# A four-layer graph network: layer 1 and the input norm moved forward, low lanes weighed on ScalarE, searches further ahead

## The chip, the core and the metric

The kernel runs on one core of a Trainium2 chip. It is launched once and computes all 16 graphs. The metric is the device time of that launch in microseconds (us). Engines carry the names of the profile: PE is TensorE (matmuls; PEld are its weight loads), DVE is VectorE, ACT is ScalarE, POOL is GpSimd and SP is SyncE. In this kernel POOL issues only indirect DMAs (a gather or scatter of 128 rows by a column of indices) and SP issues all other DMAs.

## The reference

Sixteen graphs of 1024 nodes and 64 features, each with a weighted adjacency matrix, go through four layers. Every layer adds its output to its input, and begins with `h = max(layernorm(x), 0)`.

```python
# layer 0
out = einsum('bij,bjo->bio', adj, h @ weight) + bias
# layer 1
e = f_src[:, :, None] + f_dst[:, None, :]      # from leaky_relu(h @ W) @ a
dj = 0.8 * adj + 0.2 * e
attention = softmax(where(dj > 0, dj, -1e12), axis=1)
out = relu(einsum('bij,bjo->bio', attention, h @ W))
# layer 2 (hyperbolic attention)
x_local = logmap(x_i, x_j, c)
att = sigmoid(einsum(..., att_W) + att_b) * adj
out = proj(expmap(einsum('bij,bijd->bid', att, x_local), x, c), c)
# layer 3: quantiles over the neighbours that are left after thinning
s = sort(where(nd[..., None], h[:, None, :, :], inf), axis=2)
agg = 0.25 * q(0.25) + 0.5 * q(0.5) + 0.25 * q(0.75)   # between two sorted lanes each
out = (relu((h + agg) @ W1 + b1) @ W2 + b2) * mask
```

Layer 3 is the unusual one. Each node has a list of neighbours whose features are sorted, one feature apart from the other, and three quantiles are read from the sorted list.

## The kernel before, in words

**Streams and a planner.** The kernel is written as generators ("streams") that issue instructions. A planner runs while the program is built. It books each instruction on a model of the engines (`Plan`), and at each point it steps the stream that is ready and least far in its share of VectorE work. `yield [tile]` means "go on when the plan has this tile finished", `yield (tile,)` the same and 12 us later (`LATE_US`), and `yield lambda: ...` waits for a state of another stream. These waits exist only while building; what the chip sees is a fixed order for each engine, recorded in `Queue.call` at L190, so that nearly every instruction of the profile has line L190 and is told by its tiles. On the chip, real semaphores hold each instruction until its tiles are there.

**heads** (`heads`, `fast0`, `fast1`, `fast2`) goes over the graphs. `fast0` is layer 0: norm, then for 8 column tiles of the adjacency matrix the matmuls `pa<-adj,h`, and the edge flags `ng<-adj` on VectorE. `fast1` is layer 1: its norm, transposes and small matmuls (the preamble), and then the attention over 8 tiles (`d<-adj,fsr,fd`, `ex`). `fast2` is layer 2: 16 half-row units of pairs (`pd`, `pl` on PE, `u_g` and `u_z` on ScalarE and VectorE, transposes `pw`, `w<-pw,adj`, and `pm`). **moves** then makes the step of layer 2 (`move_steps`, some 40 tiny VectorE instructions that begin with `dot_pr` and `c_hm`), stores x and the norm for layer 3 (`s_hd`) in DRAM, and raises `headed`. `heads` of the next graph does its layer 0 meanwhile, but waits for `headed` ahead of all of layer 1, as layer 1's tiles take the memory of the step's (`moving.close()`).

**places** thins the edges, ranks each row's neighbours (a prefix sum on PE) and sorts the nodes by their number of neighbours. It scatters the rank rows, so sorted, to DRAM (`s_vp`, 8 indirect DMAs a graph on POOL). **weigh** makes the weight of each sorted lane (`wlow`, `wd`).

**fetches** finds the neighbours. For 128 nodes it loads rank rows (`row`, three buffers, two loads ahead), searches them on VectorE (`max_index`, FIND_INDEX8 in the profile) for eight ranks at once, and queues one gather from `s_hd` for each lane: 116 for the rows with few neighbours (`la`) and 48 for the 80 "hub" nodes (`hg`) a graph. What it looks for, 32 ranks for low rows or 8 for hubs, is copied by ScalarE behind the row's 1024 entries, so that a rank which the row lacks is found in the pad (it then gathers a row of zeros). `Issue` puts the queued gathers in POOL's order, and the scatters between them. `AHEAD_US = 16.0` says how far ahead of POOL's planned work a search is made. The first searches of a graph wait for `headed`.

**hubs** and **lows** sort by max and min on VectorE (`ha`/`hb`, `la`/`lb`), with copies of idle lanes on ScalarE. For low rows there are seven groups (`LOW`) of 31 to 7 lanes; after the sort VectorE multiplies the lanes that a quantile can touch by `wlow` (one instruction a group) and sums them in halves into `aggl`:

```python
v = a[:pn, :, l0:l1, :]
nc.vector.tensor_tensor(v, v, wlow[...].to_broadcast([pn, nt, l1 - l0, C]), ALU.mult)
```

**finish** stores the sums, gathers them back in node order (`ga`, 8 indirect DMAs on POOL), runs layer 3's two matmuls (`hid`, `py`) and stores the result.

Three states `st[b % 3]` bound how many graphs are under way. Streams share VectorE by `HEADS_US, HUBS_US, LOWS_US = 127.0, 82.0, 93.0`.

Of the kernel before, what the change touches and what calls it, by code (L numbers as in the profile page):

```python
# [29 lines left out]
C = 64  # L30
# [40 lines left out]
AHEAD_US = 16.0  # L71
LA = (1, 3, 2)
LATE_US = 12.0
HEADS_US, HUBS_US, LOWS_US = 127.0, 82.0, 93.0
PAD = 32
# [268 lines left out]
def tile_gnn_stack(  # L344
# [76 lines left out]
    seek = scp.tile([P, PAD], F16, name="seek")  # L421
    nc.gpsimd.iota(seek, pattern=[[2, PAD]], base=1, channel_multiplier=0, allow_small_or_imprecise_dtypes=True)
    iolane = scp.tile([P, 288], F32, name="iolane")
    nc.gpsimd.iota(iolane, pattern=[[1, 288]], base=0, channel_multiplier=0, allow_small_or_imprecise_dtypes=True)
    nseek = scp.tile([P, PAD], F32, name="nseek")
    nc.gpsimd.iota(nseek, pattern=[[-2, PAD]], base=-1, channel_multiplier=0, allow_small_or_imprecise_dtypes=True)
# [941 lines left out]
    def fast0(feed, xt, xn, ng):  # L1368

        with tc.tile_pool(name="f0", bufs=1) as sp, tc.tile_pool(name="f0p", bufs=1, space=PSUM) as ps:  # L1370
            h = sp.tile([P, NT, C], F32, name="h")
            yield from norm_steps(h, xt, sp, "ln_xc")
            pa = ps.tile([P, HN], F32, name="pa")
            po = ps.tile([P, 2, NT, C], F32, name="po")
            for hf in range(2):
                nc.tensor.matmul(po[:, hf, 0:4, :], ones[0:1, :], b0r[0:1, None, :].to_broadcast([1, 4, C]), start=True, stop=False)

            def others(J):
                blk = ng[:, J, J * P:(J + 1) * P]
                nc.vector.tensor_tensor(blk, blk, noteye, ALU.mult)  # L1380

            yield [h]
            for J in range(NT):
                a = feed.next()
                yield [a, h]
                halves(pa, h[:, J, :], a, J)
                nc.vector.tensor_scalar(ng[:, J, :], a, 0.0, None, ALU.is_gt)
                if J:
                    others(J - 1)
            others(NT - 1)  # L1390
            yield [pa]
            ga = sp.tile([P, HN], F32, name="ga")
            nc.scalar.copy(ga, pa)
            yield [ga]

            for k in range(4):
                for hf in range(2):
                    rs = slice(64 * hf, 64 * hf + 64)
                    nc.tensor.matmul(po[:, hf, k, :], ga[rs, k * P:(k + 1) * P], w0d[rs], start=False, stop=(k == 3))
            yield  # L1400
            v = "p (h k) c -> p h k c"
            nc.vector.tensor_tensor(xn.rearrange(v, h=2), po[:, :, 0:4, :], xt.rearrange(v, h=2), ALU.add)

    def fast1(feed, xt, xn):
        with tc.tile_pool(name="f1", bufs=1) as sp, tc.tile_pool(name="f1w", bufs=2) as wp, \
                tc.tile_pool(name="f1p", bufs=2, space=PSUM) as ps:
            h = sp.tile([P, NT, C], F32, name="h")
            yield from norm_steps(h, xt, sp, "ln_xc")

            cat = sp.tile([P, N], F32, name="cat")  # L1410
# [29 lines left out]
            hp = sp.tile([P, NT, C], F32, name="hp")  # L1440
            nc.scalar.copy(hp, ph)
            yield [fsr, fd]
# [67 lines left out]
            r = sp.tile([P, HN], F32, name="r")  # L1510
# [306 lines left out]

    def heads(io, feed, T, st):

        xa = load_x(io, 0)  # L1820
        moving = None
        for b in range(B):
            s = st[b % 3]
            nes = ExitStack()
            ng = nes.enter_context(tc.tile_pool(name="n1", bufs=1, side="right")).tile([P, NT, N], F16, name="ng")
            yield [xa]
            yield from fast0(feed, xa, xa, ng)
            T.flagged[b] = ng, nes.enter_context(tc.tile_pool(name="np", bufs=2, space=PSUM, side="right"))
            yield lambda: T.headed >= b
            if moving:  # L1830
                moving.close()
            yield [xa]
            yield from fast1(feed, xa, xa)
            yield [xa]

            def ranked():
                yield lambda: T.ranked > b
                nes.close()

            moving = ExitStack()  # L1840
            tp = moving.enter_context(tc.tile_pool(name="mv", bufs=1))
            args = yield from fast2(feed, xa, s.bad, ranked, tp)
            T.moves[b] = xa, args, moving.enter_context(tc.tile_pool(name="mw", bufs=1))
            if b + 1 < B:
                xa = load_x(io, b + 1)
            yield []
        yield lambda: T.headed >= B
        moving.close()
# [47 lines left out]
    def places(b, s, sp, T):  # L1896
# [119 lines left out]
        nc.vector.tensor_scalar(s.place, rk, float(N - 1), 0.5, ALU.add, ALU.mult)  # L2016
        for I in range(NT):
            issue.rows.append(lambda I=I: nc.gpsimd.indirect_dma_start(
                out=s.vp, out_offset=bass.IndirectOffsetOnAxis(ap=s.place[:, I:I + 1], axis=0),
                in_=vr[:, I, :], in_offset=None))  # L2020
# [158 lines left out]
    class Tail:  # L2179

        def __init__(self, es):
# [3 lines left out]
            self.dp = es.enter_context(tc.tile_pool(name="yd", bufs=2, space=bass.MemoryType.DRAM))  # L2185
            self.placed = self.ranked = self.headed = self.turned = self.hubbed = self.lowed = self.finished = 0
            self.out = [0, 0, 0]
            self.flagged, self.got, self.weights, self.sums, self.moves = {}, {}, {}, {}, {}

# [58 lines left out]
        def fetches(self, b, s):  # L2248
# [31 lines left out]
            def load():  # L2280
# [3 lines left out]
                row = wp.tile([P, N + PAD], F16, tag="row", name="row", bufs=3)  # L2284
                if i < 6:
# [12 lines left out]
                    nc.scalar.copy(row[:pn, N:N + 8], hseek[:pn, t, :])  # L2298
                else:
# [3 lines left out]
                    nc.scalar.copy(row[:pn, N:], seek[:pn])  # L2303
                rows[i] = row

            load()
            load()
# [26 lines left out]
            def search(row, n, what, pn):  # L2334
                ix = wp.tile([P, 8], U32, tag="ix", name="ix", bufs=8)
                nc.vector.max_index(ix[:pn], what, row[:pn, 0:n])
                return ix
# [6 lines left out]
            def fetch_hub(k):  # L2344
# [3 lines left out]
                for h in range(2):  # L2348
# [3 lines left out]
                    ix = search(rows[2 * k + h], N + 8, hseek[:pn, k, :], pn)  # L2352
# [4 lines left out]
            def fetch_low(k):  # L2357
# [5 lines left out]
                for t in range(t0, t0 + nt):  # L2363
# [3 lines left out]
                    yield lambda: len(issue.queue) <= 24  # L2367
# [9 lines left out]
                    for l0 in range(0, d, 8):  # L2377
                        if d - l0 <= 3:
                            yield [sm]
                            ix = wp.tile([P, 8], I32, tag="ix", name="ix", bufs=8)  # L2380
# [52 lines left out]
        def lows(self, b):  # L2433
# [3 lines left out]
            wlow = self.weights[b][0]  # L2437
            aggl = self.sums[b, 1] = self.bp.tile([P, LOWT, C], F32, name="aggl", bufs=2)
            for k, (t0, nt, d, few) in enumerate(LOW):
# [7 lines left out]
                v = a[:pn, :, l0:l1, :]  # L2447
                nc.vector.tensor_tensor(v, v, wlow[:pn, t0:t0 + nt, l0:l1][:, :, :, None].to_broadcast([pn, nt, l1 - l0, C]), ALU.mult)
                yield
# [6 lines left out]
                self.out[(k > 0) + (k > 4)] -= 1  # L2456
# [3 lines left out]
        def finish(self, b, s):  # L2460
# [19 lines left out]
            yield [ad]  # L2480
# [10 lines left out]
            hid = bp.tile([H, N], F32, name="hid")  # L2491
# [9 lines left out]
            for t in range(NT):  # L2501
                nc.tensor.matmul(py[:, t, :], hid[:, t * P:(t + 1) * P], w2s, start=False, stop=(t == NT - 1))
            yield [py]
# [50 lines left out]
    with ExitStack() as es:  # L2554
# [5 lines left out]
        def each(f, *more):  # L2560
            for b in range(B):
# [6 lines left out]
                  Stream(plan, each(lambda b: moves(b, st[b % 3], T)), lag=-1.0),  # L2568
                  Stream(plan, heads(io, Feed(io), T, st), HEADS_US),
# [67 lines left out]
```

## Time and profile before

| | |
|---|---|
| median of 23 runs | 5237.44 us (5214.2 to 5259.39) |
| profiled execution, its own time | 5231.94 us |
| its span, first to last instruction | 5230.2 us |
| mean granted TensorE clock | 0.597 |
| first edge flags (`ng<-adj`) of graphs 0, 1, 2, 15 | 33, 274, 530, 4500 us |
| first step instruction (`c_hm`) of graph 15 | 4786 us |
| gathers `la` and `hg`: first, last | 295, 5188 us |
| gathers `la` of graph 9 and of graph 10 begin | 3025, 3325 us |

Busy times are unions of records. A group's mean is the length of one record, and records of neighbouring instructions on an engine overlap by a little, so the distance from start to start is the better price when instructions follow each other closely; the prediction says which it uses. The first 500 us fill the pipeline: layer 3 of the first graph can't begin before its layer 2 is done. From about 530 to 4786 us graphs follow each other every 306 us, with layer 0 to 2 of one graph beside layer 3 of the one or two before. The last 440 us hold what is left of layer 3. "issue" behind an indirect DMA is time in which POOL waits for nothing that the profile shows. `DVE ix` as the releaser of a gather is the search that found its indices.

### The profile page before, as it was taken

What the parts mean: (1) busy time and instruction counts of PE and PEld (TensorE: products, weight loads), DVE (VectorE), ACT (ScalarE), POOL (GpSimd) and SP (SyncE); (2) the same over time, 40 slices, a digit from 0 to 9 for tenths busy, and PEclk for the clock granted to TensorE, in tenths of its full rate; (3) what the DMA queues carried; (4) which work ended last, traced back from release to release, by engine and by line L of the source; (5) the groups of instructions that cost most, each with busy time, mean ns of one, the idle gap of its engine ahead of it and who ended that gap; (6) DMA issues with size and microseconds to landing.
All of it is one profiled execution on the core that took longest, in us unless ns stands there. A gap on an engine that the chain in (4) does not pass through costs nothing. (4 is left out here: it accounts for less than half of the span.)

```text
span 5230.2 us, 59422 instructions
## 1 busy us (share of the span) xinstructions
PE 3470.0 (66%) x13331; PEld 1893.2 (36%) x13332; DVE 4679.7 (89%) x12742; ACT 3152.9 (60%) x9317; POOL 3810.5 (73%) x2906
## 2 busy tenths in 40 slices
PE   6967686766867567686866768686767867674010
PEld 2525243333524334352433435243343524333000
DVE  3368999899999999999999999989999999999866
ACT  4566666657566665756667575666757566675222
POOL 0057778788777777777777777777777777678886
PEclk8566656556565655656556565755666565665555
DMA  2133333333333233333333333332333333232120
GB/s 86 55 92 83 95 82 86 84 93 77 84 96 81 76 98 89 76 85 96 77 79 100 89 76 85 97 77 77 93 96 79 81 98 77 77 102 42 38 43 14
DMA packets 458515, 419.30 MB, mean 80 GB/s; under 512 B 215811, under 2 KB 349411, under 8 KB 458148
## 3 DMA queue, kind: packets, MB, share of 16 engines
q1 hardware_dynamic: 351652, 295.93, 19.5%
q0 software_dynamic: 106496, 119.49, 12.0%
q8 instruction: 108, 1.77, 0.1%
q14 instruction: 259, 2.12, 0.1%
HBM read 363.98 MB, written 50.54 MB: 79 GB/s over the span
## 5 line engine op out<-in xcount | busy, mean ns | idle before, releaser
L190 POOL DMA_INDIRECT la<-s_hd,ix x1856 | 2517.2, 1356 | 837.0 <-issue 489.8
L190 POOL DMA_INDIRECT hg<-s_hd,ix x768 | 1005.1, 1309 | 235.0 <-issue 208.5
L190 DVE TENSOR_TENSOR lb<-la 128x128 f32<-128x128 f32 (+14 forms) x1760 | 674.5, 434 | 65.8 <-DMA la<-s_hd,ix 43.8
L190 DVE TENSOR_TENSOR la<-lb 128x256 f32<-128x256 f32 (+11 forms) x1856 | 694.0, 428 | 32.1 <-ACT lb L190 26.9
L190 DVE TENSOR_TENSOR hb<-ha 128x128 f32<-128x128 f32 (+36 forms) x1632 | 655.2, 442 | 34.6 <-ACT ha L190 33.6
L190 DVE TENSOR_TENSOR ha<-hb 128x64 f32<-128x64 f32 (+36 forms) x1568 | 620.2, 435 | 21.9 <-ACT hb L190 21.3
L190 PE MATMUL pd<-near,dist 66*128 66x512 f32 x512 | 468.7, 1016 | 10.9 <-DVE u_g L190 6.3
L190 PE MATMUL pv<-wtile,krow 8*128 8x512 f16 x512 | 295.5, 577 | 249.0 <-ACT d L190 152.8
L190 PE MATMUL pl<-near,lead 65*128 65x512 f32 x512 | 459.5, 998 | 0.0
L190 PEld LDWEIGHTS pm<-hn,w 128*128 128x128 f32 x2048 | 431.0, 317 | 71.2 <-issue 59.0
L190 PE MATMUL pm<-hn,w 128*128 128x65 f32 x2048 | 435.7, 399 | 5.6 <-DVE w L190 5.6
L190 ACT ACTIVATE u_g<-pd,gxc 128x512 f32<-128x512 f32 x256 | 175.4, 685 | 317.9 <-PE pd L190 317.6
L190 PE MATMUL pw<-ident,u_z 128*128 128x128 f32 x1024 | 261.8, 407 | 158.0 <-DVE u_z L190 157.9
L190 POOL DMA_INDIRECT s_vp<-vr,s_place x128 | 147.3, 1150 | 266.5 <-DVE s_place L190 170.1
L190 PE MATMUL pa<-adj,h 128*64 128x512 f32 x512 | 163.3, 764 | 266.8 <-ACT h L190 210.4
L190 PEld LDWEIGHTS <-ng 128*128 128x128 f16 x2048 | 170.3, 127 | 467.8 <-issue 467.8
L190 ACT COPY ha<-hb 128x4 f32<-128x4 f32 (+22 forms) x1264 | 253.1, 273 | 119.9 <-DVE hb L190 90.8
L190 ACT COPY hb<-ha 128x32 f32<-128x32 f32 (+24 forms) x1280 | 272.5, 287 | 79.4 <-DVE ha L190 76.1
L190 ACT COPY lb<-la 128x64 f32<-128x64 f32 (+6 forms) x784 | 196.0, 298 | 181.5 <-DVE la L190 113.3
L190 PE MATMUL pv<-wt,ng 128*128 128x128 f16 x2048 | 301.9, 300 | 0.0
L190 ACT ACTIVATE u_z<-u_z,c_gs 128x512 f32<-128x512 f32 x256 | 183.4, 717 | 191.4 <-DVE u_z L190 187.7
L190 PEld LDWEIGHTS pw<-ident,u_z 128*128 128x128 f32 x1024 | 199.4, 226 | 248.9 <-issue 237.4
(300 smaller groups left out, 7901.0 us busy)
## 6 DMA issues: line engine op xcount, KB each, us to landing
adj<-in_adjt SPq DMA_DIRECT2D x384, 512.0 KB
la<-s_hd,ix POOLq DMA_INDIRECT x1856
row<-s_vp SPq DMA_DIRECT2D x112, 256.0 KB
hg<-s_hd,ix POOLq DMA_INDIRECT x768
wb<-wd SPq DMA_DIRECT2D x32, 342.0 KB
row<-s_vp SPq DMA_DIRECT2D x192, 28.0 KB
row<-s_vp SPq DMA_DIRECT2D x192, 24.0 KB
x<-in_x SPq DMA_DIRECT2D x16, 256.0 KB
```

The source lines that it names most:

```text
L190: r = f(*a, **k)
```

## The change

1. **Low lanes.** A new stream `totals` takes over from `lows`. For each group ScalarE multiplies every lane of every tile by its weight (a Copy ACTIVATE of 128x64 with a pointer scale), 79 a graph in place of 7 VectorE instructions; VectorE still makes the sums. Groups 1 to 6 are written to a new tile `lw`, of which there is one; a lock (`taken`) keeps it for one group at a time, and layer 3's hidden tile `hid` shares it. `LOWS_US` is 78.
2. **Searches.** `AHEAD_US` is 40, the queue may hold 40 gathers for low rows too (24 before), and there are 16 index buffers (8 before). Rows lie in four fixed tiles, three loads ahead. What is looked for is written behind each of them once, at the start: the hubs' 24 ranks and then the low rows' 32, so `PAD` is 56, a hub search reads 1048 entries (1032 before) and a low one 1080 (1056).
3. **Layer 1.** `fast1` takes its tiles from the other end of memory and calls `cleared()`, which waits for `headed`, only after the preamble and ahead of the attention. `hp` shares the buffer of `h`, and `r` that of `cat`.
4. **Input norm.** A new stream `first_norms` loads x and makes layer 0's norm ahead of `heads`.
5. `heads` waits ahead of layer 2 until graph b - 3 is finished; the scatters and the gathers of `finish` are queued 12 us later than the plan has their tiles.

```diff
-AHEAD_US = 16.0
+AHEAD_US = 40.0
...
-HEADS_US, HUBS_US, LOWS_US = 127.0, 82.0, 93.0
-PAD = 32
+HEADS_US, HUBS_US, LOWS_US = 127.0, 82.0, 78.0
+PAD = 56
+ROWS = 4
...
-    def fast0(feed, xt, xn, ng):
+    def fast0(feed, xt, xn, ng, h):
...
-            h = sp.tile([P, NT, C], F32, name="h")
-            yield from norm_steps(h, xt, sp, "ln_xc")
...
-    def fast1(feed, xt, xn):
-        with tc.tile_pool(name="f1", bufs=1) as sp, tc.tile_pool(name="f1w", bufs=2) as wp, \
+    def fast1(feed, xt, xn, cleared):
+        with tc.tile_pool(name="f1", bufs=1, side="right") as sp, ExitStack() as es, \
...
+            yield from cleared()
+            wp = es.enter_context(tc.tile_pool(name="f1w", bufs=2))
...
+    def first_norms(b, io, T):
+
+        yield lambda: T.headed >= b - 1 and T.entered >= b
+        xa = load_x(io, b)
+        yield [xa]
+        h = io.tile([P, NT, C], F32, name="h0")
+        yield from norm_steps(h, xa, io, "ln_xc")
+        T.normed[b] = xa, h
+        yield []
...
+            def cleared():
+                yield lambda: T.headed >= b
+                if moving:
+                    moving.close()
+
             yield [xa]
-            yield from fast1(feed, xa, xa)
+            yield from fast1(feed, xa, xa, cleared)
...
+            yield lambda: T.finished >= b - 2
             moving = ExitStack()
...
+        yield (s.place,)
...
+            self.rows = [self.bp.tile([P, N + PAD], F16, name=f"row{k}") for k in range(ROWS)]
+            for row in self.rows:
+                nc.vector.tensor_copy(row[:, N:N + 24], hseek.rearrange("p t l -> p (t l)"))
+                nc.vector.tensor_copy(row[:, N + 24:], seek)
...
-                    nc.scalar.copy(row[:pn, N:N + 8], hseek[:pn, t, :])
...
-                    nc.scalar.copy(row[:pn, N:], seek[:pn])
...
-            load()
-            load()
+            for _ in range(ROWS - 1):
+                load()
...
-                    ix = search(rows[2 * k + h], N + 8, hseek[:pn, k, :], pn)
+                    ix = search(rows[2 * k + h], N + 24, hseek[:pn, k, :], pn)
...
-                    yield lambda: len(issue.queue) <= 24
+                    yield lambda: len(issue.queue) <= 40
...
-                v = a[:pn, :, l0:l1, :]
-                nc.vector.tensor_tensor(v, v, wlow[:pn, t0:t0 + nt, l0:l1][:, :, :, None].to_broadcast([pn, nt, l1 - l0, C]), ALU.mult)
...
+        def totals(self, b):
...
+                if k:
+                    yield lambda: not self.taken
+                    self.taken = True
+                    o, s0 = self.bp.tile([P, nt * (l1 - l0) * C], F32, tag="lw", name="lw"), l0
+                    o = o.rearrange("p (t l c) -> p t l c", t=nt, c=C)
+                yield [a]
+                for i in range(nt * (l1 - l0)):
+                    t, l = i // (l1 - l0), l0 + i % (l1 - l0)
+                    nc.scalar.activation(o[:pn, t, l - s0, :], a[:pn, t, l, :], AF.Copy, scale=wlow[:pn, t0 + t, l:l + 1])
+                    if i % 8 == 7:
+                        yield []
...
-            yield [ad]
+            yield (ad,)
...
-            hid = bp.tile([H, N], F32, name="hid")
+            yield lambda: not self.taken
+            self.taken = True
+            hid = bp.tile([P, N], F32, tag="lw", name="hid")[:H]
...
+                  Stream(plan, each(T.totals), lag=-1.0),
+                  Stream(plan, each(lambda b: first_norms(b, io, T)), lag=-1.0),
```

## The prediction

> **What bounds the kernel now.** I read the page's busy line and slices first, then the waits of GpSimd and VectorE in the steady part (830 to 4790 us), then the timeline where one graph's gathers end and the next begin, and the groups by form for prices.
>
> ```profile
> PE 3470.0 (66%) x13331; PEld 1893.2 (36%) x13332; DVE 4679.7 (89%) x12742; ACT 3152.9 (60%) x9317; POOL 3810.5 (73%) x2906
> ...
> DVE  3368999899999999999999999989999999999866
> ACT  4566666657566665756667575666757566675222
> POOL 0057778788777777777777777777777777678886
> ```
>
> VectorE is at nine tenths or more in 31 of 40 slices; most of its 550 idle us lie in the first four and the last three. GpSimd looks free at 73%, but is not:
>
> ```profile
> POOL la L190 <- issue: 400.2, 1313, 0.3
> POOL hg L190 <- issue: 168.8, 554, 0.3
> POOL la L190 <- DVE ix L190: 118.7, 12, 16.1
> ...
> POOL la L190 <- ACT row L190: 49.8, 7, 13.3
> ```
>
> Each of the 180 indirect DMAs of a graph (116 for low rows, 48 for hubs, 8 scatters, 8 gathers back) has 0.3 us of issue behind it that no kernel edit here removes. With 1.32 us for one (the four groups' 3805 us over 2880), a graph costs GpSimd about 180 x 1.62 = 292 us. The steady period is 305.9 us (the first edge-flag instruction of graph 2 stands at 530, that of graph 15 at 4500). The rest is real waiting: 118.7 + 49.8 + 14.3 (a la gather behind ACT's sigmoid) + some 35 (scatters) = 217 us over 13 graphs, 16.7 us each. Where it lies:
>
> ```profile
> 3009.64 0.96 POOL L190 DMA_INDIRECT la<-s_hd,ix  x1 [0.30 <-issue]
> 3024.84 0.96 POOL L190 DMA_INDIRECT la<-s_hd,ix  x1 [14.23 <-DVE ix L190]
> ```
>
> That is the graph boundary: the first search of the new graph stands behind `headed`, which VectorE reached at 3023. So two engines are nearly level: GpSimd at 289 + 17 of waiting, VectorE at 284.7 us of work a graph + 21.2 (12 of waits, the rest stretched records). At the end GpSimd decides: graph 15's gathers run from 4876 to 5188, and 42 us of closing follow.
>
> **The parts.** *The multiplication by the weights leaves VectorE.* Seven instructions a graph, 112 in all.
>
> ```profile
> L190 DVE FIND_INDEX8 ix<-seek,row 128x8 uint32<-128x1056 f16 x208 | 259.3, 1248 | 0.0
> ...
> L190 DVE FIND_INDEX8 ix<-hseek,row 128x8 uint32<-128x1032 f16 x64 | 78.3, 1223 | 0.0
> ...
> L190 DVE TENSOR_TENSOR lb<-lb,wlow 128x1344 f32<-128x1344 f32 x16 | 25.0, 1564 | 0.4
> ```
> ```profile
> 3194.31 1.56 DVE L190 TENSOR_TENSOR lb<-lb,wlow 128x1344 f32<-128x1344 f32 x1
> 3195.79 0.68 DVE L190 TENSOR_TENSOR w<-pw,adj 128x512 f32<-128x512 f32 x1
> ```
>
> The seven rows sum to 101.6 us. Records overlap: the next one starts 1.48 us after the first, not 1.56, so 112 x 0.084 = 9.4 comes off and 92.2 us are freed. *Longer search rows* give some back: 1056 against 1032 elements is 1248 against 1223 ns, so 25 ns for 24. The low searches grow by 24 (224 x 25 ns = 5.6 us), the hub ones by 16 (96 x 17 ns = 1.6 us). Net: VectorE has **85.0 us** less. The tree sums keep their number and sizes. Layer 3's hidden tile now shares the weighed tile's buffer: at most one group (16 x 0.251 = 4 us) of waiting a graph, with other streams beside it: 0 to 64 us, I take 0, as a plan that sees the lock orders it.
>
> *On ScalarE* the seven become 79 instructions of 128x64 with a pointer scale, 1264 in all. The nearest row is the same form:
>
> ```profile
> L190 ACT ACTIVATE hs<-hp,rs 128x64 f32<-128x64 f32 x128 | 44.3, 346 | 64.9 <-DVE rs L190 62.7 <-DVE ha L190 1.5 <-DVE z L190 0.6
> ```
>
> Alone it takes 346 ns; back to back the forms with a 128x64 output start 0.25 us apart (the timeline has hs at 3059.58 and the next instruction at 3059.83; the median of 109 such is 0.251). So 1264 x 0.251 = 317 us, at most 1264 x 0.346 = 437. 224 seed copies of 0.11 us leave (25 us); the built order has 12 more table loads of 1.283 us (15 us). ScalarE goes from 3153 to about 3460 us, 66%, in the steady part from some 64% to 71%. Its free time hides it; if that cover fails, the price is rival 3's. The Trainium skill speaks against it: "ScalarE: Activation LUTs", Rules for kernel authors, gives add and multiply to VectorE, as faster per element. This trace agrees on the price (317 against 92 us), not on the advice, as VectorE is full and ScalarE has 2077 us free. The same page's formula (What ACT_TABLE_LOAD costs) would give 186 + 53 + 93 - 93 = 239 ns packed, an estimate of 302 us.
>
> *Layer 1 ahead, input norm ahead.* Nothing is removed, it is moved. I weighted the issue order of both builds with this trace's start-to-start times. VectorE work from one graph's first edge flag to the next falls from 284.7 to 272.6 us: 5.3 is the work removed, and some 7 slides behind the heads, where low rows are finished later. So the work behind the last step's first instruction grows from 318 to 402 us. That tail lasted 444 us with 318 of work in it, so there is room. The 15 us between the end of layer 2's pairs and the next flags vanish, since the norm is done. These waits go as well:
>
> ```profile
> DVE ln_m L190 <- DMA s_hd<-h: 29.3, 12, 2.7
> ```
>
> The layer 1 norm reuses what the step's last DMA reads; it now stands on the other side. What is late next is the attention's `d` tile, behind the same DMA, but that DMA has long landed by then: between 0 and the same 29 us; I take 0. In the first two graphs, where little else fills VectorE, the preamble (flags to attention 43 us) overlaps the step: 0 to 25 us, I take 10.
>
> *Searches far ahead, fixed rows.* No work, earlier: 40 us of queue instead of 16, three rows loaded ahead instead of two, no ScalarE copy into a row. It meets the 118.7 and 49.8 of GpSimd. In the built order the headed-check of a graph stands some 131 us of VectorE work behind the step's first instruction (59 before): the gathers of the graph before are still queued there, so the boundary gap should close. What stays is the scatters' 35 us. On SP the row loads wait for the same search as before (the row searched last), so nothing new is queued behind them; x is loaded earlier, in place of behind layer 2. The delays of 12 us on `s.place` and `ad` move two waits behind other work; I price them between -10 and +12 us (the closing `ad` wait once, at the end) and take 0.
>
> **The sum.** GpSimd floor: 305.9 - 16.7 = 289.2, with the scatters' 2.7 it is 292. VectorE: 272.6 + 21.2 - 3.1 (ln_m and one `ga` wait) = 290.7. Two nearly equal engines never mesh fully; between 292 and 305.9 I take **296**, near the floors because both were computed with today's slowdowns in. First gather at 295 - 10 = 285; 15 graphs x 296 = 4440; the last graph 312 as now (4876 to 5188); closing 42: 5079. The run lies 1.7 us above its span, and the median of the runs 5.5 above this run: 5086, rounded **5090**, 2.8% less.
>
> **Rivals.**
> 1. *GpSimd never starves and VectorE keeps up*: 285 + 15 x 292 + 305 (the last graph, its waits gone) + 42 + 7 = 5019. For: both floors. Against: scatters, and an order fixed by a plan. Its gathers run at 0.98 us when VectorE is idle and at 1.5 to 1.7 beside hub sorting, so a denser VectorE slows them.
> 2. *Only the removed work counts*: heads were never waited for, or PE holds layer 2's pairs. That stage lasts 117.5 us, PE's records fill 102 to 113 of it at a granted clock near 0.5, and VectorE's work in it falls from 110 to 99 us. If it shrinks only half way to 106 us, 14 x 5.8 = 81 us are lost: 5171. If the moves give nothing: 5237 - 85 = 5152. Together 5130 to 5227.
> 3. *Slower: ScalarE is late.* Each of 112 tree sums stands in VectorE's fixed order and now waits for ScalarE, as sort steps do today (33 waits in 22.2 us, 0.67 each: 75 us, still a gain). If each waits for one full chunk of eight (8 x 0.251 = 2.0 us), 224 us: 5314. It decides from (5237 - 5090) / 112 = 1.3 us a sum. For: ScalarE also feeds sigmoid and softmax in order, and VectorE already waits some 95 us for it in the steady part. Against: 29% free there, and the sums are a stream of their own, placed when the plan has them ready.
>
> **How the numbers follow.** Forecast (5050 to 5130) 0.42; rival 1 0.13; rival 2 0.30; rival 3 0.11; within 0.2% 0.04. A change of 0.2% (some 10 us) is about what this measurement can tell from none. Faster 0.85, same 0.04, slower 0.11. The range leaves out rival 3, the "same" case and the lower half of rival 1: 5020 to 5215.
>
> **What would show it.** VectorE near 4600 us busy, no `wlow` row on it; 1264 `wlow` ACTIVATEs near 346 ns; GpSimd's waits for `ix` and `row` under 60 us together instead of 168; the ln_m wait on `s_hd` gone; flags some 296 us apart; the tail after the last step's start near 470 us. Wrong if VectorE shows over 100 us of waits on the weighed tile, if `w<-PE pw` (6.9 us in the steady part) grows over 60, or if gathers get slower than 1.35 us.

## The result, and the profile of the changed kernel

The changed kernel takes 5341.86 us (median of 8 runs, 5334.32 to 5355.6), the kernel before 5233.97 us (median of 62 runs): a ratio of 1.0205, 95% interval 1.0189 to 1.0221. It is **slower by 2%**, where 2.8% less was forecast. The profiled execution has a span of 5336.7 us (before 5230.2) at a mean granted TensorE clock of 0.578 (before 0.597).

The page of the changed kernel, its busy line and the slices of three engines:

```profile
PE 3612.4 (68%) x13331; PEld 1980.6 (37%) x13332; DVE 4592.1 (86%) x12638; ACT 3427.8 (64%) x10369; POOL 3819.3 (72%) x2906
...
DVE  3367989999899999998989899999979899898755
ACT  4466667768575776757576775858667676754332
POOL 0057577768786877768777777678777868778886
```

VectorE lost 87.6 us of work, and yet ends later: it is busy for 86% of the span instead of 89%, and at nine tenths or more in 24 slices instead of 31. Its idle time grew from 550 to 745 us, by 195. In VectorE's account that is the whole loss: -88 + 195 = +107 us, the difference of the two spans. Where it lies is shown by a table of busy time in three stages (start to 830 us, then to the first step instruction `c_hm` of graph 15, then to the end). First the kernel before, then the changed one; the columns are the stretch, its length, and busy time and instructions of PE, PEld, DVE, ACT and POOL, then the granted clock, DMA share and GB/s.

```profile
0.00:830.00 830.00, 611.40 (x2422) 333.13 (x2425) 588.91 (x1547) 488.83 (x1266) 429.45 (x355) 0.64 0.30 81
830.00:4786.00 3956.00, 2825.01 (x10823) 1542.58 (x10819) 3765.87 (x10258) 2538.01 (x7519) 3031.22 (x2343) 0.60 0.34 86
4786.00:5231.00 445.00, 33.58 (x88) 17.43 (x88) 324.90 (x939) 126.10 (x534) 349.84 (x210) 0.50 0.16 31
```
```profile
0.00:830.00 830.00, 632.68 (x2398) 346.37 (x2400) 563.35 (x1520) 500.31 (x1323) 391.22 (x349) 0.62 0.29 80
830.00:4759.00 3929.00, 2927.93 (x10800) 1607.44 (x10799) 3617.98 (x9929) 2720.90 (x8230) 2979.12 (x2262) 0.58 0.33 85
4759.00:5337.00 578.00, 51.82 (x135) 26.75 (x135) 410.75 (x1190) 206.60 (x817) 448.99 (x297) 0.50 0.17 33
```

Read the third pair, DVE. In the middle stage 148 us of work left, but the stage is only 27 us shorter: idle time went from 190 to 311 us. In the last stage there are 86 us more work (low rows that slid behind the heads) and 47 us more idle time: 445 became 578 us. Fewer POOL instructions in the middle (2262 against 2343) and more at the end (297 against 210) say the same of the gathers: they fell behind and were made up at the end.

What VectorE waited for over the whole span, changed kernel (total us, times, longest us):

```profile
DVE lb L191 <- ACT la L191: 74.2, 23, 7.9
DVE lb L191 <- ACT lw L191: 72.8, 13, 12.4
DVE lb L191 <- DMA la<-s_hd,ix: 62.7, 4, 27.5
DVE w L191 <- PE pw L191: 62.4, 37, 5.8
...
DVE lw L191 <- ACT lw L191: 29.9, 22, 3.4
```

and the same rows of the kernel before:

```profile
DVE w L190 <- PE pw L190: 50.9, 28, 5.2
DVE lb L190 <- DMA la<-s_hd,ix: 43.8, 6, 14.3
...
DVE lb L190 <- ACT la L190: 15.7, 13, 9.5
```

The three rows with ACT are nearly all the weighing: 177 us, of which 14 stand behind ScalarE's copies of idle lanes, as all of the 16 us before do. The two at `lb` are not the sums. They are mostly the first sort instruction of the next group, which needs the one `lb` buffer while ScalarE still reads the sorted lanes of group 0 or 1 from it. The timeline shows one (start, duration, engine, instruction, in brackets the idle time before it and what ended it):

```profile
3344.41 3.00 ACT L191 ACTIVATE lw<-lb,wlow 128x64 f32<-128x64 f32 x12
...
3347.45 1.16 DVE L191 TENSOR_TENSOR lb<-la 128x448 f32<-128x448 f32 x2 [5.25 <-ACT lw L191]
...
3366.57 1.28 DVE L191 FIND_INDEX8 ix<-seek,row 128x8 uint32<-128x1080 f16 x1
...
3368.59 2.51 POOL L191 DMA_INDIRECT la<-s_hd,ix  x1 [40.32 <-ACT ng L191]
```

The last line is the longest wait of GpSimd in the steady part, and it is not at a graph's boundary. The gather is the first of low group 4, which needs one of three `la` buffers. These come free as the groups before it are weighed, and the search of the third line is put behind that. GpSimd's waits between 830 and 4790 us:

```profile
POOL la L191 <- issue: 426.5, 1278, 23.5
POOL hg L191 <- issue: 200.2, 540, 19.2
POOL la L191 <- ACT ng L191: 51.8, 2, 40.3
...
POOL hg L191 <- PE pg L191: 28.4, 2, 19.4
POOL hg L191 <- DVE ix L191: 28.4, 1, 28.4
```

Of the boundary's rows of before (118.7 behind `ix`, 49.8 behind `row`) 13.0 us are left; the 28.4 behind `ix` here are a hub gather's. The releasers alone don't tell all: the two rows called issue hold real waits too, the longest 23.5 and 19.2 us, where the longest was 0.3 before. Counted by a gather's place in its graph (gaps over the 0.31 us of issue, from the trace), GpSimd waited 122 us at first gathers of a graph and 61 at group 4 before, and 57 at first gathers, 111 at group 4 and 92 at the third hub group after (the first graph's first gather left out). All its waits together went from 232 to 313 us.

### The profile page after: what moved, and what is told of

Its sections match the earlier page's. It is cut to its first block, busy times and chain, and to the rows that moved or that the text cites. A ratio compares the mean times of both kernels' runs of the same rounds, so it can differ in the third digit from the quotient of the medians.

```text
span 5336.7 us, 59224 instructions
## 1 busy us (share of the span) xinstructions
PE 3612.4 (68%) x13331; PEld 1980.6 (37%) x13332; DVE 4592.1 (86%) x12638; ACT 3427.8 (64%) x10369; POOL 3819.3 (72%) x2906
## 5 line engine op out<-in xcount | busy, mean ns | idle before, releaser
L191 POOL DMA_INDIRECT la<-s_hd,ix x1856 | 2469.5, 1331 | 825.4 <-issue 530.1
L191 POOL DMA_INDIRECT hg<-s_hd,ix x768 | 1036.5, 1350 | 326.9 <-issue 246.9
L191 PE MATMUL pd<-near,dist 66*128 66x512 f32 x512 | 494.6, 1068 | 24.9 <-ACT lead L191 19.0
L191 PE MATMUL pl<-near,lead 65*128 65x512 f32 x512 | 486.8, 1053 | 0.0
L191 PEld LDWEIGHTS pm<-hn,w 128*128 128x128 f32 x2048 | 452.5, 330 | 80.2 <-issue 68.9
L191 PE MATMUL pm<-hn,w 128*128 128x65 f32 x2048 | 454.1, 412 | 4.3 <-DVE w L191 4.2
L191 PEld LDWEIGHTS pw<-ident,u_z 128*128 128x128 f32 x1024 | 211.3, 234 | 253.8 <-issue 245.9
L191 PE MATMUL pd<-ng,ident 128*128 128x512 f16 x256 | 128.0, 500 | 233.5 <-ACT ng L191 218.8
L191 DVE FIND_INDEX8 ix<-seek,row 128x8 uint32<-128x1080 f16 x224 | 284.3, 1272 | 0.0
```

The lines of the kernel that those rows point to most:

```text
L191: r = f(*a, **k)
```

## The experiments

Four theories stood against each other. (1) ScalarE weighs too late, and VectorE's next group waits. (2) The heads moved ahead take VectorE from the sorts, whose buffers then come free late. (3) The searches moved ahead stand in VectorE's way. (4) GpSimd's queue of gathers sets the end, and each part only moves its waits. A fifth came out of the runs: the order as a whole, which a planner writes anew for every edit, costs as much as any part.

In the table, VectorE's work is the page's busy time, idle is the span less that, "for ScalarE at `lb`, `lw`" the part of it that stands ahead of writes to these tiles, and GpSimd's wait the sum of the gaps between its first and last gather that exceed the issue of 0.31 us. All are of profiled executions; ratios are of timed ones, each against runs of the kernel before that were timed together with it.

| kernel | ratio (95% interval) | VectorE work | idle | for ScalarE at `lb`, `lw` | GpSimd's wait |
|---|---|---|---|---|---|
| before | 1 | 4680 | 550 | 16 | 232 |
| after | 1.0205 (1.0189 to 1.0221) | 4592 | 745 | 177 | 313 |
| c_only_2 | 1.0280 (1.0231 to 1.0329) | 4567 | 814 | 219 | 441 |
| b_only_2 | 1.0383 (1.0359 to 1.0407) | 4699 | 724 | 14 | 441 |
| a_only_2 | 1.0293 (1.0268 to 1.0317) | 4695 | 697 | 1 | 344 |
| no_c_2 | 1.0385 (1.0330 to 1.0440) | 4698 | 737 | 20 | 379 |
| weigh_dve | 1.0179 (1.0130 to 1.0228) | 4672 | 659 | 32 | 241 |
| full_wait | 1.0283 (1.0230 to 1.0336) | 4597 | 781 | 86 | 384 |
| lows78 | 1.0111 (1.0086 to 1.0135) | 4684 | 598 | 14 | 239 |
| no_weigh | 1.0126 (1.0100 to 1.0152) | 4582 | 709 | 5 | 207 |
| fewer | 1.0364 (1.0328 to 1.0400) | 4694 | 720 | 18 | 811 |
| fewer_after | 1.0285 (1.0250 to 1.0320) | 4588 | 797 | 184 | 686 |
| lows93 | 1.0969 (1.0931 to 1.1006) | 4594 | 1145 | 126 | 770 |
| fetch163 | 1.0295 (1.0256 to 1.0335) | 4597 | 791 | 232 | 321 |

The first and the last set of runs were timed where the kernel before itself took 5866 and 5850 us; their largest VectorE wait is for `w`, released by something that the trace calls remote, which no other run shows. What it is stays open. (One expectation below names late loads of the adjacency matrix; the traces don't settle that.) Their ratios stand with the kernels and aren't mixed with the others.

**One part alone: c_only, b_only, a_only, and a second time as c_only_2, b_only_2, a_only_2.** To the kernel before is added only the weighing on ScalarE (c), only layer 1 and the input norm ahead (b), or only the searches ahead with fixed rows (a, with 8 index buffers):

```diff
+        def totals(self, b):           # c, with LOWS_US 78
...
+            yield from fast1(feed, xa, xa, cleared)   # b, with first_norms
...
+AHEAD_US = 40.0                        # a, with ROWS = 4, PAD = 56
```

> The kernel before with the weighing alone moved to ScalarE (totals stream, the lw tile, the shared hidden tile, LOWS_US 78). Theory 1 (the single lb buffer makes VectorE wait until ScalarE has weighed the group before): slower than before, 5270 to 5350 us, with lb<-ACT lw and lb<-ACT la waits of 100 us or more. Theory 2 (heads moved forward leave low rows and gathers late): faster, about 5150, as only 85 us of VectorE work go.

> The kernel before with layer 1 and the input norm moved forward, and the gate on finished graphs ahead of layer 2; weighing and searches as before. Theory 1: faster or the same, 5150 to 5235. Theory 2: slower, 5300 or more, with the last graph's first gather after 4950 us instead of 4876.

> The kernel before with the searches alone changed (AHEAD_US 40, queue of 40, four fixed row tiles, pad 56), with 8 index buffers as before, since 16 do not fit beside the rest. Theory 1: within 1% of before, GpSimd's waits for ix and row fall from 168 to under 80 us. Theory 3 (searching ahead fills GpSimd's queue with gathers whose buffers are not free, and the ready ones stand behind them): slower, 5290 or more, GpSimd's waits for ScalarE and PE grow.

> The weighing alone moved to ScalarE, a second time, as the first call met a chip on which the kernel before took 5866 us (its adjacency loads landed late) instead of 5234. Theory 1 (VectorE waits for ScalarE at the single lb buffer): ratio to before above 1.005, 5270 to 5350 us where before takes 5234, with lb<-ACT lw and lb<-ACT la waits of 100 us or more. Theory 2 (heads moved forward are the cause): faster, about 5150.

> Layer 1 and the input norm moved forward alone, a second time, since the first call met a chip on which the kernel before took 5866 us. Theory 2 (heads moved forward make it slow): 5300 to 5400, first gather of the last graph after 4950 us, waits of gathers for buffers (on ScalarE and PE) in place of waits for searches. Otherwise 5150 to 5230.

> The searches alone changed (8 index buffers), a second time for the same reason. Theory 3 (queueing far ahead puts gathers whose buffers are not free in front of ready ones): 5300 or more, GpSimd's waits for ScalarE and PE grow. Otherwise 5180 to 5240, with less waiting for ix and row.

Measured: 1.0142, 1.0416 and 1.1124 in the first set; 1.028, 1.0383 and 1.0293 in the second (5382, 5430 and 5391 us; the first two lie above the ranges expected). Each part alone is slower. The weighing alone saves 113 us of VectorE's work and adds 264 of idle time, 203 of it ahead of `lb` and `lw`. Not all of its 150 us need be the weighing's: its `LOWS_US` of 78, alone, costs 50 (lows78, below). The heads ahead move GpSimd's wait from the first gather of a graph (122 to 13 us) to group 4 (61 to 259). The searches ahead, alone, do the contrary: 278 us at first gathers. The three losses sum to 9.6%, the whole change loses 2.1%, so they are not costs of the parts that add up.

**All but the weighing: no_c, no_c_2.** The changed kernel with the weighing put back into `lows` on VectorE:

```diff
-                    nc.scalar.activation(o[:pn, t, l - s0, :], a[:pn, t, l, :], AF.Copy, scale=wlow[:pn, t0 + t, l:l + 1])
+                nc.vector.tensor_tensor(v, v, wlow[:pn, t0:t0 + nt, l0:l1][:, :, :, None].to_broadcast([pn, nt, l1 - l0, C]), ALU.mult)
```

> The changed kernel with the weighing back on VectorE inside lows as before (LOWS_US 78 kept). Theory 1: clearly faster than the changed one, 5130 to 5220. Theories 2 and 3: stays slower than before, 5300 or more.

> The changed kernel with the weighing back on VectorE inside lows (LOWS_US 78 kept), a second time for the same reason. Theory 1: faster than before, 5130 to 5220. Theories 2 and 3 (searches far ahead block GpSimd's queue): slower than before, 5300 or more.

Measured: 1.0425 in the first set, 1.0385 in the second. ScalarE's lateness is no longer there, and it is slower still, so that lateness is not the whole cause.

**The weighing by VectorE within the change: weigh_dve.** The stream `totals`, the tile `lw` and the order's streams stay; one VectorE instruction a group takes the place of ScalarE's.

```diff
-                for i in range(nt * (l1 - l0)):
-                    t, l = i // (l1 - l0), l0 + i % (l1 - l0)
-                    nc.scalar.activation(o[:pn, t, l - s0, :], a[:pn, t, l, :], AF.Copy, scale=wlow[:pn, t0 + t, l:l + 1])
+                nc.vector.tensor_tensor(o[:pn, :, l0 - s0:l1 - s0, :], a[:pn, :, l0:l1, :], wlow[...].to_broadcast([...]), ALU.mult)
```

> The changed kernel with the totals stream, the lw tile and all else kept, but VectorE making each group's weighing in one instruction into the same tile. Theory 1: the lb waits on ScalarE vanish (some 150 us) for 92 us of VectorE work, so 5200 to 5290, faster than the changed kernel. Theory 2 or 3: as slow as the changed kernel or slower, 5340 to 5430.

Measured: 5329.96 us, which can't be told from the changed kernel. It lies between the ranges of the two expectations. This is the pair that splits the account. VectorE's waits in weigh_dve over the whole span:

```profile
DVE lb L191 <- DMA la<-s_hd,ix: 85.5, 5, 26.4
DVE ga L191 <- DMA ga<-ad,s_place: 60.5, 7, 16.0
...
DVE lb L191 <- ACT la L191: 24.5, 13, 10.7
```

Everything else of the change costs 109 us of idle time (550 to 659) with 8 us of work saved; the largest growth is ahead of `lb`, for gathers (43.8 to 85.5), and of `ga` (28.4 to 60.5). 24 us of these belong to this variant alone: VectorE now writes `lw` itself and waits for the matmuls that read the shared hidden tile (`lw` behind `PE py`, 23.7 us, 4 times). Putting the weighing on ScalarE then saves 80 us of work (4672 to 4592) and adds 86 us of idle time (659 to 745): nothing is left.

GpSimd's account of weigh_dve needs hardly any waits. Its first gather comes 12 us later than in the kernel before, its waits grew by 9 us, and its gathers and scatters themselves last 73 us longer (3789.4 to 3862.7 us), mostly for those of the hubs. Together that is 94 us at the last gather, of 100 at the end. First the kernel before, then weigh_dve:

```profile
L190 POOL DMA_INDIRECT hg<-s_hd,ix x768 | 1005.1, 1309 | 235.0 <-issue 208.5
```
```profile
L191 POOL DMA_INDIRECT hg<-s_hd,ix x768 | 1103.6, 1437 | 274.6 <-issue 231.8
```

**The buffer held longer in the plan: full_wait.** The planner frees `lb` and the `la` buffer only when it has the weighed tile finished, so that it puts other work ahead of the next group:

```diff
-                self.weighed.add((b, k))
-                if k:
-                    self.out[1 + (k > 4)] -= 1
                 yield [o]
+                self.weighed.add((b, k))
+                if k:
+                    self.out[1 + (k > 4)] -= 1
```

> The changed kernel, but the plan lets the next group start to sort (and the next gather take the buffer) only when it has the weighing finished, not when it is issued. Theory 1: VectorE's waits lb<-ACT fall from 147 to under 70 us and the time to 5200 to 5290. Theory 2 or 3: within 0.5% of the changed kernel.

Measured: 5384.33 us, in neither expectation's range, though VectorE's waits at `lb` fell to 10 us. The waits for ScalarE at `lb` and `lw` together fall from 177 to 86 us, and idle time rises all the same, from 745 to 781: the waits that were mended came back elsewhere, part of them at `la` (48.1 us behind ScalarE's writes to it, against 9.6).

**Only the order, lows78, and only less work, no_weigh.** lows78 is the kernel before with a smaller share of VectorE for the low sorts; no instruction is added or removed. no_weigh leaves the multiplication out.

```diff
-HEADS_US, HUBS_US, LOWS_US = 127.0, 82.0, 93.0     # lows78
+HEADS_US, HUBS_US, LOWS_US = 127.0, 82.0, 78.0
...
-                nc.vector.tensor_tensor(v, v, wlow[...].to_broadcast([...]), ALU.mult)     # no_weigh
```

> The kernel before with LOWS_US 78 instead of 93 and nothing else: no instruction is added or removed, only the planner's order changes. Theory 4 (GpSimd's queue is the chain that sets the end, and any order in which its gathers meet buffers that are not yet free, or searches not yet made, costs time, whatever work goes): the time moves by over 1%, probably slower, 5290 to 5400, with GpSimd's gaps grown by about as much. Theory 1 (the weighing on ScalarE is the cause by itself): within 0.5% of before.

> The kernel before with the seven multiplications by the weights left out, so that the sums are unweighted; VectorE has 92 us less to do. If VectorE's work sets the time: 5140 to 5160. Theory 4: 5200 to 5300, as the gathers set the end and their gaps are not made shorter by it.

Measured: 5287.89 and 5296.93 us. Another order of the same instructions costs 50 us, and 98 us less work (4680 to 4582) with nothing put in its place makes the kernel slower by 1.3%. Theory 4 named the time of lows78 but not the way: GpSimd's waits grew by 7 us only, and its gathers' own time by 43 (3789 to 3832). One wait of no_weigh, over the whole span:

```profile
DVE w L190 <- PE pw L190: 127.0, 57, 7.3
```

Before, this wait was 50.9 us. Taking an instruction out changed the order that the planner wrote, and in the new one layer 2 stands more often with nothing beside it.

**GpSimd relieved: fewer, fewer_after.** By then I held theory 4: first gather, durations, issue gaps and waits of GpSimd sum to every run's time. But any engine's account does that. The test is to give GpSimd less to do, in the kernel before and in the changed one:

```diff
-            def fetch(dst, ix, l, pn):
+            def fetch(dst, ix, l, pn, plain):
+                if plain:
+                    issue.queue.append(lambda: nc.sync.dma_start(dst, s.hd[0:pn, :]))
+                    return
```

> The kernel before with 208 of its 2624 neighbour gathers (the eighth lane of each hub row, the lanes from 24 on of the first low group; 13 a graph) replaced by plain loads of 128 fixed rows that SP issues at the same places, so these lanes hold other data; VectorE's work is the same. If GpSimd's queue sets the time, it has 208 x (1.32 + 0.305) = 338 us less to do and VectorE (284.7 us of work a graph and some 12 us of waits) becomes the bound: a period near 297 us, 5040 to 5150 in all. If VectorE or ScalarE set the time: within 0.5% of the kernel before, 5210 to 5265, with GpSimd's waits some 300 us longer.

> The changed kernel with the same 208 gathers replaced by plain loads of fixed rows on SP (these lanes hold other data). If GpSimd's queue and the balance around it cost the change its gain, the gain comes out once GpSimd is relieved: VectorE has 85 us less work than in the kernel fewer, so it lands below that, 4980 to 5100. If ScalarE's weighing holds VectorE up by itself, it stays 80 us or more above the kernel fewer. If neither engine is relieved by it, 5300 to 5350.

Measured: 5420.49 and 5382.67 us, outside every range that was expected. GpSimd's gathers and issue gaps take 394 us less (4662 to 4268), and the kernel before became 3.6% slower: giving GpSimd less to do did not give time. GpSimd only waits longer at the boundary, and VectorE has more idle time in places that the kernel before keeps covered. Kernel fewer, first GpSimd's wait between 830 and 4790 us, then VectorE's over the whole span:

```profile
POOL la L190 <- DVE ix L190: 696.3, 13, 55.5
```
```profile
DVE w L190 <- PE pw L190: 132.3, 58, 5.2
DVE c_bb L190 <- ACT sq L190: 101.2, 16, 11.4
```

`c_bb` is a link of the step's chain of tiny instructions: 101.2 us against 10.6 before. As I read it, the sorts that stood between these links were done earlier, as their gathers were, and the chain lies bare. This is less than a refutation of theory 4. The edit made the planner write a new order too, and in it GpSimd waits 811 us and surely isn't the limit; whether it is in the kernel before, where it waits 232 us, this pair can't say. With that load the changed kernel is the faster of the two, by 38 us (less than an order alone can move): what the change is worth depends on the order that it meets.

**The order within the change: lows93, fetch163.** The old share for the low sorts, and a planner that is told the measured distance between gathers.

```diff
-HEADS_US, HUBS_US, LOWS_US = 127.0, 82.0, 78.0     # lows93
+HEADS_US, HUBS_US, LOWS_US = 127.0, 82.0, 93.0
...
-    HOP, FETCH, LAND, RATE = 0.06, 1.55, 2.2, 185e3     # fetch163
+    HOP, FETCH, LAND, RATE = 0.06, 1.63, 2.2, 185e3
```

> The changed kernel with the old share of VectorE for the low sorts (93 in place of 78 in the planner's LOWS_US); no instruction is added or removed. If the loss is one of balance, GpSimd's waits for low buffers (111 us at a graph's group 4 and 92 at its third hub group in the changed kernel) fall below 100 together and some of it comes back at the graph boundary: 5250 to 5320. If ScalarE's lateness costs it, the share does not matter: 5325 to 5360.

> The changed kernel, planned with 1.63 us from gather to gather (1.325 us for one and 0.305 of issue in its trace) in place of 1.55, so that the plan's GpSimd is no longer ahead of the chip's by some 14 us a graph; no instruction is added or removed. If the plan's drift places the heads too early and the low rows too late, 5220 to 5290. If it doesn't matter, 5310 to 5370.

Measured: 5740.18 and 5389.92 us, outside all four ranges; neither order gained. The share matters more than anything else tried: 398 us for 15 us of share, with VectorE's work unchanged. In lows93 the hubs come late. GpSimd waits 688 us at the third hub group, and VectorE for the end of each graph; first GpSimd's longest rows, then VectorE's, whole span:

```profile
POOL hg L191 <- PE pt L191: 352.5, 7, 65.8
...
POOL hg L191 <- PE pg L191: 137.6, 2, 82.9
```
```profile
DVE ga L191 <- DMA ga<-ad,s_place: 209.2, 12, 23.5
DVE y L191 <- ACT y L191: 170.4, 14, 13.3
```

In fetch163 group 4's wait grew from 111 to 223 us and the third hub group's fell from 92 to 46.

**Only the two groups that hold `lb`, on VectorE: mixed, c_mixed.** If the 147 us at `lb` are the loss, weighing groups 0 and 1 on VectorE (40 us) should win most of it back. mixed is that within the whole change, c_mixed with the weighing as its only part.

```diff
+                held = a is not o
...
+                if held:
+                    nc.vector.tensor_tensor(o[:pn, :, l0 - s0:l1 - s0, :], a[:pn, :, l0:l1, :], wlow[...].to_broadcast([...]), ALU.mult)
+                else:
```

> The changed kernel, but the two low groups whose sorted lanes end in lb (33 of the 79 ScalarE instructions a graph) are weighed by one VectorE instruction each, as before. If the waits for lb cost the time by themselves, 147 - 16 = 131 us of VectorE's idle time go and 40 us of work come (25.0 and 15.4 in the rows of before): 5336 - 131 + 40 = 5245, within 5225 to 5270. If they only stand where other waits would, as weighing all seven on VectorE suggests (5330): 5305 to 5360.

> The kernel before with the weighing part of the change alone, and groups 0 and 1 weighed by VectorE. Weighing alone gave 5382 with 101 + 8 us of waits for lb, against 14 with the same share of VectorE and no such part (lows78, 5288). If these waits cost the time by themselves: 5382 - 95 + 40 = 5327, and with the 110 us of sums that wait for lanes not yet weighed gone too, as ScalarE is less loaded, 5220 to 5290, which would be the first to come near the kernel before. If they take the place of others: 5340 to 5400.

Measured: ratios of 1.041 (1.0303 to 1.0516) and 1.0147 (1.006 to 1.0234), timed where the kernel before took 5850.48 us, so the expectations in us can't be read against them. c_mixed has a partner that met much the same conditions (5866 us), c_only, at 1.0142 (1.0073 to 1.0212). VectorE's waits over the whole span, first c_only, then c_mixed:

```profile
DVE lb L190 <- ACT la L190: 119.7, 35, 12.1
DVE lw L190 <- ACT lw L190: 102.7, 45, 4.8
```
```profile
DVE lw L190 <- PE py L190: 68.0, 7, 11.6
...
DVE lw L190 <- ACT lw L190: 41.1, 30, 4.3
...
DVE lb L190 <- ACT la L190: 17.9, 17, 8.9
```

163 us of the waits for ScalarE are gone for 51 us of work more, and the time stands where it stood. But 68.0 us came new, which c_only doesn't have: VectorE, now the writer of `lw` in group 1, waits for the matmuls that read the shared hidden tile. What is left is 163 - 51 - 68 = 44 us, less than the two intervals can show (some 65 us for the difference), so this pair doesn't decide whether the waits for `lb` cost the time. mixed has no partner (the whole change did not run there), and says nothing. No version beat the kernel before.

## Why the prediction was wrong

**VectorE's work: right.** 85.0 us less was forecast, 87.6 measured; a low search takes 1272 ns (1248 before), as forecast. VectorE's work in the steady part fell from 290.4 to 277.5 us a graph, by 12.9 (12.1 forecast).

**ScalarE's work: right, its cover wrong.** The changed kernel's row of the largest form:

```profile
L191 ACT ACTIVATE lw<-la,wlow 128x64 f32<-128x64 f32 x640 | 160.1, 339 | 35.0 <-DVE la L191 34.8
```

339 ns alone, 12 in 3.00 us packed: the prices used. The lock on `hid` cost VectorE nothing, as forecast, and ScalarE 10.8 us (`lw` behind `PE py`); where VectorE writes `lw` it cost more, 24 us in weigh_dve and 68 in c_mixed. ScalarE came to 3428 us (3460 forecast). "Its free time hides it" failed: a share of free time says nothing of when it is free. The mark set for this was over 100 us of waits on the weighed tile: the waits for the weighing come to 163 us, but only 29.9 of them stand at `lw`, and 133 at `lb`. Rival 3 had the mechanism and nearly the time (5314), and the wrong place: not 112 sums late (29.9 us), but some 36 waits of 4 us (23 + 13, the few copies among them) for the one buffer that a group leaves to the next. And in weigh_dve they are gone and the time is the same, so rival 3 isn't the whole answer. With the weighing on ScalarE the change takes 5342 us, with it on VectorE 5330: these two can't be told apart, so no run here decides on the page's advice that the prediction weighed.

**Layer 1 and the norm ahead: right in what goes, wrong in what it gives.** The `ln_m` wait on `s_hd` is gone, `d` waits 9.8 us instead, and the 15 us between the step's start and the next edge flags are gone (-1). From the flags to layer 2 it took 172.5 us before and takes 194.9 now, layer 2 itself 118.0 and now 107.7: 305.4 and 302.0 in all (means of graphs 2 to 14). As I read it, the heads are one chain with low sorts put between its links; what was taken out of the chain was filled with other streams' instructions. The first gather came at 305 us, not 285.

**Searches ahead: right in direction at the boundary, wrong as a gain.** 168 us of `ix` and `row` became 41, under the 60 forecast; by their place in the graph, the waits at first gathers were halved (122 to 57 us). But the waits did not go, they moved. What is late next was named as the scatters (35 us); those grew from 42 to 51 us between the first and the last gather. The larger part was the third hub group (0 to 92 us) and group 4 (61 to 111), which by the program wait for buffers that VectorE's sorts free.

**The sum: the step that failed.** "Two nearly equal engines never mesh fully; between 292 and 305.9 I take 296" took the sums of work as floors and the waits removed as time gained: 296 leaves GpSimd some 7 us of waiting a graph above the 289.2, in place of 16.7. Its work was nearly right: gathers and issue take 4662 us before and 4671 after, some 293 us a graph in both. The waiting was wrong: 313 us in all, some 19 a graph. In the heads' frame the period is 302.0 us: 277.5 of VectorE's work and 24.5 of idle time, where before it was 290.4 and 15.0. (The prediction reads these as 284.7 and 21.2 of a period of 305.9; its own flags, 530 and 4500 us, give 305.4.) The 12.9 saved became 9.5 of waiting. In the frame of the prediction's sum, first gathers of a graph are (4985 - 305) / 15 = 312.0 us apart, not 296: gathers fell 10 us a graph behind the heads. Term by term: first gather +20, fifteen periods +240, the last graph -10 (302 for 312), closing +7 (49 for 42), together 257 of the 258 us between 5079 and 5337. The tail after the last step's start was forecast near 470 us with 402 of VectorE's work; it had 411, and took 578, as 167 us of waiting stand in it.

**What is shown, and what stays open.** Shown: the work left VectorE as forecast, and its idle time grew by 195 us against 88 saved; 109 of idle time stand there with the weighing on VectorE too (weigh_dve); no part of the change gains alone; less work does not by itself give time, not on VectorE (no_weigh) and not on GpSimd (fewer); and another order of the same instructions costs 48 to 398 us (lows78, fetch163, lows93). Argued, not shown: that the kernel before is at a point where its shares and prices fit, and nearly any new order idles more. A rival stands beside it. Between its first and last neighbour gather GpSimd is in a gather or its issue for 95% of the time in the kernel before, and for 94 to 96% in the changed kernel, lows78, no_weigh and weigh_dve. In the last three its gathers' own time grew by 43 to 73 us, so slower gathers may set the time there; no run kept the order and changed only the gathers. Thirteen other orders, the changed kernel's among them, were timed where the kernel before takes some 5235 us, and none came below it. Open: what in the new order costs the time, and whether an order exists in which the change wins. Neither a fourth `la` buffer nor a second `lb` was tried.

## What to carry to other kernels

Where a planner writes a fixed order, an edit is two things, its own work and a new order for all the rest. First time an edit that only changes the order (here 1% for one share in the kernel before, 7.5% in the changed one), for below that size no sum of parts can be trusted. Work taken from the fullest engine is a gain only if what it waits for comes earlier as well: look for the single buffers and the in-order queues that its next instruction needs. An engine's account that sums to the time proves nothing. Lightening that engine is the better test, but where the planner answers it with a new order, it tests that order as well: both lighter kernels here came out slower.

## What the runs showed of the hardware that was not expected

A gather's duration depends on what VectorE does beside it. The gathers of the kernel before, sorted by what VectorE does for most (70%) of a gather's first 0.9 us:

| VectorE beside the gather | gathers | mean us | longest us |
|---|---|---|---|
| idle for 70% | 137 | 0.98 | 1.43 |
| searches `ix<-seek,row` | 115 | 1.04 | 1.50 |
| `w<-pw,adj` (one operand in PSUM) | 63 | 1.08 | 1.62 |
| `u_z<-pl,u_g` (one operand in PSUM) | 35 | 1.15 | 1.43 |
| `u_z<-u_z,u_g` (both operands in SBUF) | 38 | 1.14 | 1.63 |
| sort instructions (both operands in SBUF) | 1413 | 1.48 | 23.0 |

The Trainium skill, "GPSIMD Engine Reference", section Key points, says that GpSimd shares its SBUF interfaces with VectorE, with contention for VectorE instructions that have two SBUF inputs. The trace agrees for the sorts, and adds the size; `u_z<-u_z,u_g`, which has two such inputs as well, shows no more than `u_z<-pl,u_g`, which has one. The summed duration of the 2864 gathers and scatters between the first and the last neighbour gather ranges from 3724 us (c_only_2) to 3863 us (weigh_dve) in the kernels that issue as many.

PE was 142 us busier (3470 to 3612) with the same instructions, at a granted clock of 0.578 in place of 0.597; VectorE's wait for `pw` grew by only 11.5 us (50.9 to 62.4).
